# Adding up softmax exponentials on other engines: two accumulating DMAs at every odd step, no GpSimd addition, and VectorE's addition placed one step later

## The chip, the core and the metric

The kernel runs on one core of a Trainium2 chip: TensorE (PE; its weight loads are listed as PEld), VectorE (DVE), ScalarE (ACT), GpSimd (POOL) and SyncE (SP), each with its own queue of instructions in program order, and 16 DMA engines. The metric is device time in microseconds (us) of one launch. Before the change three runs took 2907.7, 2908.85 and 2916.73 us; the median is 2908.85 us.

## The reference

Two "metaformer" layers over an input of 2 x 256 x 64 x 64. Layer 0 has an area attention and a recurrence, layer 1 a set of small convolutions with a state-space scan and a mixture of experts. The change is in layer 0's attention alone:

```python
B, C, H, W = x.shape                        # 2, 256, 64, 64
N, hd = H * W, C // HEADS                   # 4096, 32 (HEADS = 8)
qk = _conv1x1_bn(x, w_qk, ...)
vv = _conv1x1_bn(x, w_v, ...)
pp = depthwise 5x5 convolution of vv, then batch norm
Ba, Na = (B * AREA, N // AREA)              # 8 areas of 1024 positions
...
attn = jnp.einsum('bhdn,bhdm->bhnm', q, k) * hd ** (-0.5)
attn = jax.nn.softmax(attn, axis=-1)
o = jnp.einsum('bhdm,bhnm->bhdn', v, attn)
...
return _conv1x1_bn(o + pp, w_proj, ...)
```

In each of 8 areas and 8 heads, 1024 queries attend to 1024 keys. The softmax needs, for each query, the sum of the exponentials over all 1024 keys; how this sum is put together is what changes.

## The kernel before

**Groups and steps.** A group is one area and one half of the channels (4 heads): 16 groups, 0 to 15. Each group has 16 steps t. A step handles 512 queries (`n`, the half) and 128 keys (`m`, 0 to 7), for 4 heads. The loop over all 256 steps (L567) writes the instructions out by hand in their final order; tables (`MINE`, `SMALL`, `LATE`, `AROUND`, `TAPS` and others) say which other work goes in at which step. Within a step the order is:

1. `scores` (L366): TensorE makes the scores in two PSUM tiles of two heads each (L371, L376), ScalarE takes their exponentials into two SBUF tiles of 128 x 1024 f32 (L383). They are named `sx0`, `sx1` at each fourth step (m = 0 and 4) and `ex0`, `ex1` at the others; each name has two buffers in turn.
2. `values` (L393) of the step before: TensorE multiplies its exponentials with v (L389, `av_o`).
3. `maxima` (L270) of the group to come: TensorE makes scores (L276); at even steps ScalarE stores their positive part (L288), at odd steps VectorE reduces against it (L292, four instructions). Three PSUM buffers of two banks are shared by 1 and 3.
4. The additions of exponentials, described below.
5. The taps of the 5 x 5 convolution on VectorE (L346), one to three a step.
6. Small work by table: projections for the next group (L166), their evictions, the layer norm's steps for the next area (`centre`, `square`, `variance`, `root`, `scale`), the output projection (L359), and at t = 15 `key_difference` (L264), a GpSimd subtraction of two key tiles that the next group's first `maxima` needs as `kd`. `join` (L308, L309) runs on GpSimd at t = 7 and 15. `root` (at t = 6 of a group with the first half of the channels, an "even group") is a transpose on VectorE (L199, `ln_t`), then an addition and a power on GpSimd (L202, L203); its second part comes at t = 8.

**The sums of exponentials.** Four steps (m = 0 to 3, or 4 to 7) are added into one pair of tiles, `total`, which are the `sx` tiles of the first of them. Two steps after the fourth, `sums` (L404) multiplies `total` by ones on TensorE (L389, `po`), which adds over the 128 keys; of each half of the queries, `sums` runs twice (two quads), and after the second VectorE normalises `y` (L415 to L423). Who adds what, before:

| step | first tile (heads 0 and 1) | second tile (heads 2 and 3) |
|---|---|---|
| m = 0, 4 | is the total | is the total |
| m = 1, 5 | accumulating DMA (L591) | GpSimd addition (L593) |
| m = 2, 6 | accumulating DMA | VectorE addition (L600), after the step's taps |
| m = 3, 7 | accumulating DMA | GpSimd addition |

An accumulating DMA reads `exs[0]` (512 KB), adds it to `total[0]` and writes it back. It is issued from GpSimd's queue, which stands still until the DMA before it on the same tile has landed. The GpSimd addition carries two extra waits (L595, L596), on the last score matmul of `maxima` and on the latest marked VectorE instruction before it, so that it starts beside VectorE's reductions, which read PSUM. `mark` records, all over the code, which VectorE instruction came last.

Of the kernel before, what the change touches and what calls it, by code (L numbers as in the profile page):

```python
# [14 lines left out]
ALU = mybir.AluOpType  # L15
# [78 lines left out]
def area_attention(tc, sh, ap):  # L94
# [9 lines left out]
    nc, x = tc.nc, sh.x  # L104
# [3 lines left out]
    with ExitStack() as ctx:  # L108
# [12 lines left out]
        w = {}  # L121
# [12 lines left out]
        held, xns, vhs, vts, qs, ks, kds, mxs, accs, ys, nms = ({} for _ in range(11))  # L134
# [4 lines left out]

        minus_half = cp.tile([P, 1], F32, name="minus_half")  # L140
        nc.gpsimd.memset(minus_half, -0.5)
        latest = [None]

        def mark(op):

            latest[0] = op.ins

        def wide():
            return ps1.tile([P, 2, 512], F32, name="ps", tag="ps")

# [3 lines left out]
        def temp(name, A):  # L154

            if (name, A) not in held:
                if early[0] is not None and A == 0:
                    held[name, A] = early[0].tile([P, NA], F32, name=name)
                else:
                    held[name, A] = p3.tile([P, NA], F32, name=name, tag="tmp")  # L160
            return held[name, A]
# [8 lines left out]
        def area(A):  # L170
            b, a = AREAS[A]
            return x[:, :, b, a * NA : (a + 1) * NA]
# [11 lines left out]
        def centre(A, c, at=FULL):  # L184
            if A not in xns:
                xns[A] = p1.tile([P, 2, NA], F32, name="xn")
            mark(nc.vector.tensor_tensor(xns[A][:, c, at], area(A)[:, c, at], temp("pm", A)[:, at], ALU.subtract))

        def square(A, c, at=FULL):
            nc.scalar.activation(temp(f"sq{c}", A)[:, at], xns[A][:, c, at], AF.Square)  # L190
# [4 lines left out]
        def root(A, part, at=FULL):  # L195
            n = (at.stop - at.start) // 32
            if part == 0:
                turned = temp("ln_t", A)[:, at]
                mark(nc.vector.transpose(turned, temp("var", A)[:, at]))  # L199
                t = turned.rearrange("p (k i) -> p k i", i=32)[:, :, 0]  # L200
                y = held["root", at.start] = p1.tile([P, NA // 32], F32, name="root")[:, :n]
                nc.gpsimd.tensor_scalar(y, t, 1e-6, None, ALU.add)  # L202
                nc.gpsimd.tensor_tensor(y, y, minus_half.to_broadcast([P, n]), ALU.pow)  # L203
            else:
                y = held.pop(("root", at.start))
                mark(nc.vector.transpose(
                    temp("ln_r", A)[:, at].rearrange("p (k i) -> p k i", i=32),
                    y.unsqueeze(2).to_broadcast([P, n, 32]),
                ))

        def scale(A, c, at=FULL):
            mark(nc.vector.tensor_tensor(xns[A][:, c, at], xns[A][:, c, at], temp("ln_r", A)[:, at], ALU.mult))

        def columns(t):
            return lambda k: t[:, k]
# [112 lines left out]
        def taps(A):  # L328

            vh, a = vhs[A], AREAS[A][1]  # L330
            for lower in range(2):
                for c in range(2):
                    if not lower:
                        acc = accs[A, c] = p1.tile([P, AROWS, WW], F32, name=f"acc{c}")
                        nc.vector.tensor_scalar(
                            acc, vh[:, c, 2 : 2 + AROWS], w_pe[:, c, 12:13], t_pe[:, c : c + 1], ALU.mult, ALU.add
                        )
                        yield
                    for k in range(25):
                        dy, dx = k // 5 - 2, k % 5 - 2  # L340
                        if dy == 0 and dx == 0 or (dy > 0) != lower:
                            continue
                        r0, r1 = window(dy, AROWS, AROWS * a, HH)
                        w0, w1 = window(dx, WW)
                        part = accs[A, c][:, r0:r1, w0:w1]
                        mark(nc.vector.scalar_tensor_tensor(  # L346
                            part, vh[:, c, 2 + r0 + dy : 2 + r1 + dy, w0 + dx : w1 + dx],
                            w_pe[:, c, k : k + 1], part, ALU.mult, ALU.add,
                        ))
                        yield  # L350

        def add_taps(A, c):
            y = ys[A, c]
            mark(nc.vector.tensor_tensor(y, y, accs.pop((A, c)).rearrange("p r w -> p (r w)"), ALU.add))

        def output(A, co, half):
            ps, to = bank(), area(A)[:, co, HALVES[half]]
            project(w["wpr"], co, lambda k: ys[A, k], half, ps)
            mark(nc.vector.scalar_tensor_tensor(to, ps, s_pr[:, co : co + 1], to, ALU.mult, ALU.add))  # L359

        def shift(A, co):

# [41 lines left out]
        def sums(G, n, half, exs):  # L404

            ps = bank()
            for h in range(GH):
                on_columns(ps, h, ones, exs, True, True)
            if half == 0:
                held["sum"] = p1.tile([P, 512], F32, name="sum")  # L410
                nc.scalar.copy(held["sum"], ps)
                return

            y, total = ys[GROUPS[G]][:, HALVES[n]], held.pop("sum")
            nc.vector.tensor_tensor(total, total, ps, ALU.add)  # L415
            turned = exs[0][:, 0]
            nc.vector.transpose(turned, total)
            small = p1.tile([P, 512 // 32], F32, name="small")
            nc.vector.reciprocal(small, turned.rearrange("p (k i) -> p k i", i=32)[:, :, 0])
            nc.vector.transpose(  # L420
                total.rearrange("p (k i) -> p k i", i=32), small.unsqueeze(2).to_broadcast([P, 512 // 32, 32])
            )
            mark(nc.vector.tensor_tensor(y, y, total, ALU.mult))  # L423

# [135 lines left out]
                    f(at, *a)  # L562

        pending, due, total = None, {}, None
        at_end = mybir.DependencyInfo(mybir.DependencyClass.Sync, mybir.DependencyReason.DATA)
        conv = iter(())
        for g in range(16 * len(GROUPS)):  # L567
            G, t = divmod(g, 16)
# [12 lines left out]
                values(*pending)  # L581
            works(G, t, SMALL_FIRST if new else SMALL, {})

            mm, before = None, latest[0]
            for k, at in (AHEAD_FIRST if new else AHEAD).get(t, ()):
                if G + k < len(GROUPS):
                    mm = maxima(G + k, at)
            if m % 4 == 0:
                total = exs
            else:  # L590
                nc.gpsimd.dma_start(total[0], exs[0], accum_op=ALU.add)  # L591
            if m % 2:
                add = nc.gpsimd.tensor_tensor(total[1], total[1], exs[1], ALU.add)  # L593
                if mm is not None:
                    tc.add_manual_dep(add.ins, mm.name, at_end, reason="beside the reductions")  # L595
                    tc.add_manual_dep(add.ins, before.name, at_end, reason="beside the reductions")  # L596
            for _ in range((TAPS_FIRST if A == 0 else TAPS)[c][t]):
                next(conv, None)
            if m % 4 == 2:
                mark(nc.vector.tensor_tensor(total[1], total[1], exs[1], ALU.add))  # L600
            works(G, t, FIRST if new else MINE, AROUND[c])
            if g in due:
                sums(*due.pop(g))
# [1719 lines left out]
```

## Time and profile before

| | |
|---|---|
| median of three runs | 2908.85 us |
| profiled execution | 2907.71 us, of it span 2905.9 us |
| attention, first score block to last output | about 62 to 1402 us of the span |
| PE busy, whole span | 2650.5 us (91%) |
| DVE / ACT / POOL busy | 1991.1 (69%) / 1562.2 (54%) / 1289.3 us (44%) |
| DMA queue 0 (issued from GpSimd) | 53056 packets, 225.88 MB, 30.5% of 16 engines |
| mean step in attention, from the first score blocks (L371) at 62.2 and 1375.2 us | (1375.2 - 62.2) / 255 = 5.15 us |
| accumulating DMA (L591), issue to landing | 4.5 / 4.6 / 6.3 us, min / median / max |
| GpSimd addition (L593) | 2337 / 2480 / 3080 ns |
| VectorE addition (L600) | 1215 / 1218 / 1312 ns |
| VectorE tap (L346) | 1115 / 1269 / 6770 ns |

"Busy" leaves out waiting, but a busy PE is not one at its peak. A line such as `L593 POOL TENSOR_TENSOR sx<-sx,ex ... x128 | 324.5, 2535 | 12.3 <-PE ...` reads: line, engine, operation, output and inputs, shape, how many; busy us in all and mean ns of one; idle time of the engine just before, and what ended it. In the timeline a line has start us, duration us (of a run of like instructions merged, with their count at the end), engine, line; in brackets the idle time before it and who ended it.

### The profile page before, as it was taken

What the parts mean: (1) busy time and instruction counts of PE and PEld (TensorE: products, weight loads), DVE (VectorE), ACT (ScalarE), POOL (GpSimd) and SP (SyncE); (2) the same over time, 40 slices, a digit from 0 to 9 for tenths busy, and PEclk for the clock granted to TensorE, in tenths of its full rate; (3) what the DMA queues carried; (4) which work ended last, traced back from release to release, by engine and by line L of the source; (5) the groups of instructions that cost most, each with busy time, mean ns of one, the idle gap of its engine ahead of it and who ended that gap; (6) DMA issues with size and microseconds to landing.
All of it is one profiled execution on the core that took longest, in us unless ns stands there. A gap on an engine that the chain in (4) does not pass through costs nothing.

```text
span 2905.9 us, 45896 instructions
## 1 busy us (share of the span) xinstructions
PE 2650.5 (91%) x17286; PEld 1490.6 (51%) x17286; DVE 1991.1 (69%) x3765; ACT 1562.2 (54%) x2641; POOL 1289.3 (44%) x1115
## 2 busy tenths in 40 slices
PE   7999999999999999998799999968886599999994
PEld 2223333333333333222599999933343488888873
DVE  4789888888888888879566666788897622222116
ACT  3667676676767676665244555567645522222223
POOL 1454545444554545445213000058772166666651
PEclk9999999999999999998799999989998799999995
DMA  3333443434343434445231000035552366666658
GB/s 131 66 73 74 80 81 73 81 74 81 75 79 74 80 73 81 78 79 100 80 126 65 1 1 2 1 86 150 143 149 94 113 216 232 220 229 229 221 177 348
DMA packets 86393, 321.04 MB, mean 110 GB/s; under 512 B 17608, under 2 KB 18512, under 8 KB 76432
## 3 DMA queue, kind: packets, MB, share of 16 engines
q0 software_dynamic: 53056, 225.88, 30.5%
q1 hardware_dynamic: 31872, 87.86, 9.4%
q10 hardware_dynamic: 1232, 4.25, 0.4%
q8 instruction: 139, 2.28, 0.3%
q14 instruction: 94, 0.77, 0.1%
HBM read 173.30 MB, written 43.58 MB: 75 GB/s over the span
## 4 chain that ended last, share of the span: by engine, by line
PE 74%; DVE 10%; issue 5%; DMA 4%; POOL 4%; ACT 3%; SPq 0%; DVEq 0%; POOLq 0%; ACTq 0%
PE ps L276 9%; PE ph L2069 9%; PE py L2079 8%; PE av_o L389 7%; PE z L796 7%; PE po L166 7%; PE z L808 7%; PE ps L376 6%; PE ps L371 3%; DMA sx<-ex 2%; DVE hs L1541 2%; PE yp L1551 2%; PE po L178 2%; PE po L389 2%; PE px L2057 1%
## 5 line engine op out<-in xcount | busy, mean ns | idle before, releaser
L346 DVE SCALAR_TENSOR_TENSOR acc<-vh,w_pe,acc 128x1008 f32<-128x1008 f32 (+7 forms) x384 | 534.0, 1393 | 9.5
L383 ACT ACTIVATE ex<-ps 128x1024 f32<-128x1024 f32 x384 | 372.8, 1024 | 177.2 <-PE ps L376 101.9
L591 POOL DMA_DIRECT2D sx<-ex x192 | 167.9, 875 | 594.6 <-ACT ex L383 273.5
L292 DVE CUSTOM_DVE_ANT_0 more<-ps,more 128x512 f32<-128x512 f32 x480 | 303.0, 687 | 154.6 <-PE ps L276 146.0
L2071 ACT ACTIVATE act<-ph,wt 128x256 f32<-128x256 f32 x272 | 128.8, 474 | 386.1 <-PE ph L2069 381.9
L593 POOL TENSOR_TENSOR sx<-sx,ex 128x1024 f32<-128x1024 f32 x128 | 324.5, 2535 | 12.3 <-PE ps L276 6.9
L2059 DVE COPY xt<-px 128x512 f32<-128x512 f32 x68 | 47.1, 692 | 396.7 <-PE px L2057 396.7
L2069 PE MATMUL ph<-xt,wt 128*128 128x256 f32 x1088 | 291.7, 391 | 4.7 <-ACT act L2071 3.0
L376 PE MATMUL ps<-q,k 32*128 32x512 f32 x2048 | 290.9, 607 | 0.0
L2079 PE MATMUL py<-wt,act 128*128 128x256 f32 x1088 | 278.8, 379 | 0.0
L288 ACT ACTIVATE more<-ps 128x1024 f32<-128x1024 f32 x240 | 233.1, 1025 | 30.3 <-ACT rows L320 7.8
L2069 PEld LDWEIGHTS ph<-xt,wt 128*128 128x128 f32 x1088 | 190.7, 191 | 67.0 <-DVE xt L2059 23.5
L796 PE MATMUL z<-xs,u 128*128 128x128 f32 x1872 | 224.5, 277 | 0.0
L796 PEld LDWEIGHTS z<-xs,u 128*128 128x128 f32 x1872 | 218.2, 194 | 0.2 <-issue 0.2
L2079 PEld LDWEIGHTS py<-wt,act 128*128 128x128 f32 x1088 | 202.0, 190 | 24.5
L820 ACT ACTIVATE t<-z,bias 128x128 f32<-128x128 f32 x468 | 136.3, 362 | 145.6 <-PE z L808 145.4
L389 PE MATMUL av_o<-ex,vt 128*32 128x512 f32 x1536 | 208.7, 613 | 0.2 <-ACT ex L383 0.2
L2094 POOL DMA_INDIRECT results<-y,ri x136 | 138.0, 1015 | 138.4 <-DVE y L2087 116.4
L276 PE MATMUL ps<-k,q 32*128 32x512 f32 x1088 | 186.5, 640 | 1.4 <-DVE nm L282 0.7
L808 PE MATMUL z<-xs,v 128*128 128x128 f32 x1512 | 180.1, 276 | 0.1
L808 PEld LDWEIGHTS z<-xs,v 128*128 128x128 f32 x1512 | 174.3, 192 | 0.7 <-DVE xs L827 0.7
L1548 POOL TENSOR_TENSOR cs<-hs,cs 128x1024 f32<-128x1024 f32 x63 | 148.9, 2365 | 54.4 <-DVE hs L1541 33.5
(431 smaller groups left out, 4535.8 us busy)
## 6 DMA issues: line engine op xcount, KB each, us to landing
sx<-ex POOLq DMA_DIRECT2D x192, 512.0 KB, 4.6
cs<-c_rows SPq DMA_DIRECT2D x128, 256.0 KB
y<-results SPq DMA_DIRECT2D x32, 512.0 KB
x<-xrows SPq DMA_DIRECT2D x8, 1024.0 KB
rows<-xt SPq DMA_DIRECT2D x16, 512.0 KB
out_x<-res POOLq DMA_DIRECT2D x15, 512.0 KB, 7.0
xrows<-xn SPq DMA_DIRECT2D x24, 256.0 KB
x<-in_x SPq DMA_DIRECT2D x4, 1024.0 KB
```

The lines of the kernel that those rows point to most:

```text
L276: mm = nc.tensor.matmul(tiles[h // 2][:, h % 2], qs[G, i // HM][head(h), i % HM * P : (i % HM + 1) * P], keys[head(h)], start=True, stop=T ...
L288: nc.scalar.activation(held["more"][j], tiles[j], AF.Relu)
L292: nc.vector.tensor_tensor_reduce(more, tiles[h // 2][:, h % 2], more, -1.0, 3.0e38, ALU.add, ALU.min, accum_out=nms[G][:, 0, h, i : i + 1],)
L346: mark(nc.vector.scalar_tensor_tensor(part, vh[:, c, 2 + r0 + dy : 2 + r1 + dy, w0 + dx : w1 + dx], w_pe[:, c, k : k + 1], part, ALU.mult, ...
L376: nc.tensor.matmul(tiles[h // 2][:, h % 2], k[head(h), m % HM * P : (m % HM + 1) * P], qs[G, n][head(h)], start=False, stop=True, tile_pos ...
L383: nc.scalar.activation(exs[i], tiles[i], AF.Exp, scale=HD**-0.5)
L389: nc.tensor.matmul(to[head(h)], lhs, exs[h // 2][:, h % 2], start=first, stop=last, tile_position=(0, HD * h))
L593: add = nc.gpsimd.tensor_tensor(total[1], total[1], exs[1], ALU.add)
L796: nc.tensor.matmul(z[c][:, g, :m], u[:, k, c, g], xt[:, k], start=g == GATES[0] and k == 0, stop=False, skip_group_check=True,)
L808: nc.tensor.matmul(z[c][:, g, :m], v[:, k, c, g], h[:, k], start=False, stop=k == 1, skip_group_check=True,)
L2069: nc.tensor.matmul(ph[:, hc], wt[:, at : at + P], xt[:, c], start=c == 0, stop=c == 1)
L2079: nc.tensor.matmul(py[:, j], act[:, hc, j * P : j * P + P], wt[:, at : at + C], start=hc == 0, stop=hc == NH - 1,)
```

## The change

GpSimd adds nothing any more. At odd m both tiles go by accumulating DMA, at m = 2 and 6 only the first. The second tile of m = 2 and 6 is still added by VectorE, but one step later: at the start of step m = 3 or 7, ahead of that step's `maxima` and after everything that VectorE has to do in the step before. `pending[3]` are the exponentials of the step before. The extra waits, `mark` and `latest` go with the GpSimd additions; taking away `mark(...)` around the other VectorE instructions changes none of them.

| step | first tile | second tile |
|---|---|---|
| m = 1, 5 | DMA | DMA |
| m = 2, 6 | DMA | (VectorE, in the next step) |
| m = 3, 7 | DMA | VectorE adds step 2's, then DMA adds step 3's |

```diff
-        latest = [None]
-
-        def mark(op):
-
-            latest[0] = op.ins
-
...
-        at_end = mybir.DependencyInfo(mybir.DependencyClass.Sync, mybir.DependencyReason.DATA)
...
-            mm, before = None, latest[0]
+            if m % 4 == 3:
+                nc.vector.tensor_tensor(total[1], total[1], pending[3][1], ALU.add)
             for k, at in (AHEAD_FIRST if new else AHEAD).get(t, ()):
                 if G + k < len(GROUPS):
-                    mm = maxima(G + k, at)
+                    maxima(G + k, at)
             if m % 4 == 0:
                 total = exs
-            else:
-                nc.gpsimd.dma_start(total[0], exs[0], accum_op=ALU.add)
-            if m % 2:
-                add = nc.gpsimd.tensor_tensor(total[1], total[1], exs[1], ALU.add)
-                if mm is not None:
-                    tc.add_manual_dep(add.ins, mm.name, at_end, reason="beside the reductions")
-                    tc.add_manual_dep(add.ins, before.name, at_end, reason="beside the reductions")
+            for i in ((), (0, 1), (0,), (0, 1))[m % 4]:
+                nc.gpsimd.dma_start(total[i], exs[i], accum_op=ALU.add)
             for _ in range((TAPS_FIRST if A == 0 else TAPS)[c][t]):
                 next(conv, None)
-            if m % 4 == 2:
-                mark(nc.vector.tensor_tensor(total[1], total[1], exs[1], ALU.add))
             works(G, t, FIRST if new else MINE, AROUND[c])
```

More of the change, by code (lines that the diff above doesn't have):

```diff
@@ L186, in centre @@
                 xns[A] = p1.tile([P, 2, NA], F32, name="xn")
-            mark(nc.vector.tensor_tensor(xns[A][:, c, at], area(A)[:, c, at], temp("pm", A)[:, at], ALU.subtract))
+            nc.vector.tensor_tensor(xns[A][:, c, at], area(A)[:, c, at], temp("pm", A)[:, at], ALU.subtract)
         def square(A, c, at=FULL):
@@ L198, in root @@
                 turned = temp("ln_t", A)[:, at]
-                mark(nc.vector.transpose(turned, temp("var", A)[:, at]))
+                nc.vector.transpose(turned, temp("var", A)[:, at])
                 t = turned.rearrange("p (k i) -> p k i", i=32)[:, :, 0]
@@ L205, in root @@
                 y = held.pop(("root", at.start))
-                mark(nc.vector.transpose(
+                nc.vector.transpose(
                     temp("ln_r", A)[:, at].rearrange("p (k i) -> p k i", i=32),
                     y.unsqueeze(2).to_broadcast([P, n, 32]),
-                ))
+                )
         def scale(A, c, at=FULL):
-            mark(nc.vector.tensor_tensor(xns[A][:, c, at], xns[A][:, c, at], temp("ln_r", A)[:, at], ALU.mult))
+            nc.vector.tensor_tensor(xns[A][:, c, at], xns[A][:, c, at], temp("ln_r", A)[:, at], ALU.mult)
         def columns(t):
@@ L345, in taps @@
                         part = accs[A, c][:, r0:r1, w0:w1]
-                        mark(nc.vector.scalar_tensor_tensor(
+                        nc.vector.scalar_tensor_tensor(
                             part, vh[:, c, 2 + r0 + dy : 2 + r1 + dy, w0 + dx : w1 + dx],
                             w_pe[:, c, k : k + 1], part, ALU.mult, ALU.add,
-                        ))
+                        )
                         yield
@@ L353, in add_taps @@
             y = ys[A, c]
-            mark(nc.vector.tensor_tensor(y, y, accs.pop((A, c)).rearrange("p r w -> p (r w)"), ALU.add))
+            nc.vector.tensor_tensor(y, y, accs.pop((A, c)).rearrange("p r w -> p (r w)"), ALU.add)
         def output(A, co, half):
@@ L358, in output @@
             project(w["wpr"], co, lambda k: ys[A, k], half, ps)
-            mark(nc.vector.scalar_tensor_tensor(to, ps, s_pr[:, co : co + 1], to, ALU.mult, ALU.add))
+            nc.vector.scalar_tensor_tensor(to, ps, s_pr[:, co : co + 1], to, ALU.mult, ALU.add)
         def shift(A, co):
@@ L422, in sums @@
             )
-            mark(nc.vector.tensor_tensor(y, y, total, ALU.mult))
+            nc.vector.tensor_tensor(y, y, total, ALU.mult)
         with ExitStack() as own:
```

## The prediction

> **What bounds the kernel now.** I read the busy times by stage first, then the costliest groups, the waits of TensorE, and last the timeline at the places where TensorE waits. Attention runs from about 62 us to 1400 us. The columns of the first view are the stretch, then busy time (and count) of PE, PEld, DVE, ACT and POOL, the granted clock, the DMA engines' busy share and GB/s.
>
> ```profile
> 100.00:1317.00 1217.00, 1181.88 (x7752) 368.47 (x7746) 1030.12 (x1602) 837.77 (x960) 602.72 (x463) 1.00 0.41 77
> 1317.00:1402.00 85.00, 64.07 (x387) 16.89 (x386) 69.91 (x65) 33.87 (x38) 37.10 (x26) 0.82 0.43 81
> ```
>
> Up to 1317 us TensorE is busy for 97% of the time at full clock: it is the bound, and at most 1217 - 1182 = 35 us can be won there, whatever happens on POOL. In the last group of 16 steps (1317 to 1402) it is busy for 75%, at a clock of 0.82: something else sets the pace.
>
> ```profile
> L346 DVE SCALAR_TENSOR_TENSOR acc<-vh,w_pe,acc 128x1008 f32<-128x1008 f32 (+7 forms) x384 | 534.0, 1393 | 9.5
> L591 POOL DMA_DIRECT2D sx<-ex x192 | 167.9, 875 | 594.6 <-ACT ex L383 273.5
> L593 POOL TENSOR_TENSOR sx<-sx,ex 128x1024 f32<-128x1024 f32 x128 | 324.5, 2535 | 12.3 <-PE ps L276 6.9
> ```
>
> The 128 POOL additions (L593) take 324.5 us of POOL. The taps of VectorE (L346) average 1393 ns, their median is 1269: (1393 - 1269) x 384 = 48 us lie in a few long ones, up to 6770 ns, and those stand beside POOL's two-input work. VectorE is busy for 85%, so this costs only where TensorE then waits:
>
> ```profile
> PE ps L371 <- ACT more L288: 11.9, 23, 1.0
> PE ps L371 <- DVE nm L292: 11.4, 21, 2.2
> PE po L389 <- DMA sx<-ex: 9.9, 4, 4.6
> PE ps L276 <- POOL kd L264: 9.8, 11, 2.0
> ```
>
> Us in total, times, longest. The first two return at the same steps of every group, where a step has no projection to fill the time from the last score block to its reduction, and VectorE itself waits for TensorE just before (0.7 to 1.6 us in the timeline): no addition on POOL stands in that loop. The last two can move: `kd` behind POOL's queue, and `sums` behind the accumulating DMAs.
>
> **The change part by part.** The third of each four steps has the hardest ending. At the boundary of groups 8 and 9 (start us, duration, engine, line):
>
> ```profile
> 825.03 0.85 POOL L591 DMA_DIRECT2D sx<-ex  x1 [2.45 <-DVE nm L292]
> 825.61 2.67 POOL L593 TENSOR_TENSOR sx<-sx,ex 128x1024 f32<-128x1024 f32 x1
> 827.93 1.55 POOL L264 TENSOR_TENSOR kd<-k,k 128x512 f32<-128x512 f32 x1
> 829.54 1.14 PE L276 MATMUL ps<-kd,q 32*128 32x512 f32 x8 [1.99 <-POOL kd L264]
> ```
>
> 1. *POOL's additions go, 128 DMA issues come.* An odd step spends 0.87 us (L591) in place of 2.54 (L593): 128 x 1.67 = 213 us less of POOL, which lie in POOL's idle time but for what queues behind them. That is `kd` at t = 15. ScalarE had its input (k, L247) ready at 826.18; POOL came 1.75 us later. Over the 13 boundaries into groups 2 to 14, `kd` starts 0.93, 0.88, 0.63, 1.75, 0.32 and 0.38 us after its key where POOL is late, and 0.07 to 0.08 elsewhere: 4.4 us late in sum. With two issues of 0.87 in place of 0.87 + 2.3 all are on time but this one, which keeps about 0.6: **-3.8 us**. Bounds: 0, if the DMA before it lands later by as much; -8.4, all that step 0 takes over its shortest (5.37 us), if the part that comes from taps holding up `kd` itself (1.36 us undisturbed, up to 2.29) went as well.
>
> 2. *VectorE is no longer held by L593.* Up to 1317 us I cost the 48 us at 0: VectorE's freed time turns into more waiting for TensorE. If that cover were gone, it is case C below. Behind 1317 us VectorE is the end of the chain, and it counts (part 5).
>
> 3. *Two accumulating DMAs in one step.* The DMA view for 200 to 1500 us (packets, MB, share of 16 engines; count, size, us to landing):
>
> ```profile
> q0 software_dynamic: 25200, 91.76, 37.3%
> sx<-ex POOLq DMA_DIRECT2D x175, 512.0 KB, 4.6
> ```
>
> 0.373 x 1300 / 175 = 2.77 us of all 16 engines each, 4.6 us to landing. So engines are free for 4.6 - 2.8 = 1.8 us of each, and a second one issued 0.87 us behind the first lands between 0.87 + 4.6 = 5.5 us (beside it) and 4.6 + 2.8 = 7.4 us (after it). No pair is in this trace; I take 7.0, near the upper end, because all go through queue 0. Occupancy goes from 3 x 2.77 = 8.3 to 13.9 us per four steps of 4 x 5.15 = 20.6 us: it fits. Whom does the second landing delay? ScalarE's exponential two steps later, which overwrites the tile: two steps last 8.8 to 11 us, free. VectorE's addition, which waits for it: it comes some 10 us after the issue, free. The next DMA on the first half waits only for the first landing, and starts moving 0.3 to 0.5 us later behind the rest of the second; its slack against `sums` is over 9 us. `sums` two steps after the third: over 8.6 us after the issue at t = 3, 11 and 15, free at 7.0 to 7.9. At t = 7 of even groups it is not free:
>
> ```profile
> 778.69 1.22 DVE L600 TENSOR_TENSOR sx<-sx,ex 128x1024 f32<-128x1024 f32 x1
> 781.16 0.32 POOL L202 TENSOR_SCALAR root<-ln_t 128x32 f32<-128x32 f32 x1 [4.41 <-DVE ln_t L199]
> 781.56 5.45 POOL L203 TENSOR_TENSOR root<-root,minus_half 128x32 f32<-128x32 f32 x1
> 786.98 0.93 POOL L591 DMA_DIRECT2D sx<-ex  x1
> 792.31 1.07 PE L389 MATMUL po<-sx,ones 128*32 128x512 f32 x8
> ```
>
> The power (L203) holds the DMA back, and `sums` follows 5.0 to 5.3 us after it in six groups. Its matmuls on the second half come 0.5 us later, so 5.5 to 5.8 are there for 7.0.
>
> 4. *VectorE's addition a step later.* The same 64 instructions of 1.22 us. At most steps nothing of VectorE's stands between the old and the new place, so it runs at the same time, ahead of the same reductions. At t = 6 of even groups the transpose `ln_t` stands there and goes ahead: the power begins about 1.0 us earlier (778.7 + 1.2 = 779.9 against 781.07). With part 3: 7.0 - 5.6 - 1.0 = 0.4 us in each of six groups: **+2 us** (0 by 5.5; 7.4 - 5.4 = 2.0 each, +12, if the transpose doesn't move). Queued behind the addition are the odd step's reductions, which free PSUM for TensorE; they start when TensorE has made their input, 0.4 to 2 us after the addition's end. At t = 3, 7, 11, 15 the second DMA waits for the addition, and POOL's `kd` and `join` queue behind that; the addition at t = 14 ended at 822.4, the issue would come at 825.9: covered.
>
> 5. *The last group.* It has no reductions, steps are short, and the chain runs DMA after DMA to 1355 us, then along VectorE:
>
> ```profile
> 1338.86 1.93 PE L389 MATMUL po<-sx,ones 128*32 128x512 f32 x8 [4.58 <-DMA sx<-ex]
> 1364.03 11.70 DVE L346 SCALAR_TENSOR_TENSOR acc<-vh,w_pe,acc 128x930 f32<-128x930 f32 x5
> 1383.71 3.36 DVE L354 TENSOR_TENSOR y<-y,acc 128x1024 f32<-128x1024 f32 x1
> ```
>
> On VectorE, 11.70 for five taps of 1.2 is 5.6 too long (one is the tap of 6.8), 3.36 for an addition of 1.22 is 2.1: -7.7 behind 1355 us. Against it, `sums` at t = 5 and t = 9 wait for a landing up to 2.4 us later each: +4.8, so VectorE's last stretch begins later by that. The end's `sums` has 9 us in hand (the last DMA lands at 1384.5, its use is at 1393.4), which the later chain may use up without a cost. Sum -7.7 + 4.8 = **-3 us**; bounds -7.7 (pairs land side by side) and +6, if a later landing is paid at all four sums (4 x 2.4 = 9.6) and half of VectorE's gain is lost behind it.
>
> A rule speaks against more issues from POOL. The Trainium skill, "SBUF — State Buffer", section "SBUF: two separate sides", says that GpSimd can't write a DMA's descriptors while VectorE runs in a two-port mode. Here 192 issues took 850 to 1207 ns, median 874; by the rule an issue could also wait out an operation such as L335 (818 ns), and for 15 of those the sum would be up to 12 us of POOL time, hidden; by the rows nothing.
>
> Sum: -3.8 + 2 - 3 = **-4.8 us**. The profiled execution took 2907.7 us (span 2905.9 and 1.8 around it), so it would take 2902.9; it lies 1.1 under the median of the three runs, 2908.85, from which the sum gives **2904 us**.
>
> **Rivals.** *A, forecast:* 2895 to 2909, chance 0.60. *B, the pairs get in each other's way:* the landing at t = 7 of even groups takes 9 us or more, `sums` waits over 2 us, and then the matmuls run slow: after the wait of 2.18 us at 202 us the next three took 2.31, 1.94 and 2.09 us instead of 1.24, 1.06 and 1.26 (+2.8). Six times 2.2 + 2.8 = 30 if all, half of it 15; less `kd`'s 3.8, with the last group at +4: about **2924**. It decides from 2 us of wait on. For it: no pair in the trace, and one queue. Against: 8 us of slack everywhere else. 0.18. *C, VectorE's freed time reaches TensorE:* a third of its 48 us plus part 1: **2889**. For it: TensorE's 23 us of waits for freed PSUM. Against: VectorE idles just before most of those. 0.14. *D, what `kd` wins the sums take back:* **2909**, within 1 us; the additions were off the path. 0.08.
>
> **How the numbers follow.** 0.3% (8.7 us) is about what a measurement of this kernel can tell. A straddles that bound: of its 0.60, 0.24 lie below 2900. Faster 0.24 + 0.14 = 0.38; slower B's 0.18; same 0.44. The range of 8 in 10 takes C's and B's nearer ends: 2887 to 2918; A's own is 2895 to 2909.
>
> **What would show it.** L593 gone, 320 issues at L591 of about 0.87 us; second landings 5.5 to 7.4 us after the first issue; taps' mean near 1270 ns; TensorE's wait for `kd` about 5 us in place of 9.8; step times elsewhere unchanged. Wrong, if VectorE's additions show waits for a DMA, if DMA landings exceed 9 us, or if TensorE waits for `sums` at every fourth step.

## The result, and the profile after

The changed kernel takes 2930.63 us (median of five runs, 2924.85 to 2931.59) against 2908.85 us before; the ratio is 1.0068, 95% interval 1.0049 to 1.0086. It is slower by about 22 us, where 2904 was forecast and 2887 to 2918 was the range. The profiled execution took 2930.63 us, of it span 2928.8 (before: 2907.71 and 2905.9).

Lines moved up by 6 in most of the code: the first score matmul is L365 (was L371), the second L370, the matmuls of `values` and `sums` L383, the taps L340, `kd` L258, VectorE's addition L578, the accumulating DMA L585, the transpose and the power of `root` L193, L196 and L197.

The busy times by stretch, of the changed kernel (stretch, then PE, PEld, DVE, ACT, POOL with counts, granted clock, share of the DMA engines, GB/s); the last group now lies at 1331 to 1420 us:

```profile
100.00:1317.00 1217.00, 1177.07 (x7680) 365.98 (x7680) 983.29 (x1588) 829.17 (x952) 416.02 (x458) 1.00 0.67 126
1331.00:1420.00 89.00, 68.29 (x388) 16.88 (x387) 58.02 (x65) 33.90 (x38) 24.00 (x29) 0.87 0.69 130
```

POOL gave up 187 us of work in the first stretch, VectorE 47, and TensorE, the bound, is busy for a little less than before (1177 for 1182, with 1% fewer matmuls in the stretch: 7680 for 7752). The DMA engines went from 0.41 to 0.67. Everything that was to become lighter did, and the time rose.

The costliest groups after (busy us, mean ns | idle time before them):

```profile
L585 POOL DMA_DIRECT2D sx<-ex x320 | 279.7, 949 | 812.3 <-ACT ex L377 418.8
L340 DVE SCALAR_TENSOR_TENSOR acc<-vh,w_pe,acc 128x1008 f32<-128x1008 f32 (+7 forms) x384 | 483.4, 1261 | 9.5
```

TensorE's waits in attention after, 100 to 1400 us (us in total, times, longest):

```profile
PE po L383 <- DMA sx<-ex: 20.9, 13, 3.5
PE ps L365 <- ACT more L282: 12.0, 23, 1.0
PE ps L365 <- DVE nm L286: 11.4, 21, 2.2
PE ps L270 <- POOL kd L258: 9.1, 13, 0.8
```

The two waits that were said to have nothing to do with POOL stand as they were (11.9 and 11.4 before). The one for `kd` fell by 0.7 only. The matmuls of `sums` wait for a landing 13 times in place of 4.

The DMA view of 200 to 1500 us after (packets, MB, share of 16 engines; count, size, us to landing):

```profile
q0 software_dynamic: 42208, 153.64, 62.7%
sx<-ex POOLq DMA_DIRECT2D x292, 512.0 KB, 5.4
```

0.627 x 1300 / 292 = 2.79 us of the engines each, as before; only the landing is later. In the trace, 123 of the 128 pairs were given out together (issues under 1.3 us apart). Their second DMA landed 7.3 us after the first issue in the median, 2.6 us behind the first DMA; 52 of the 123 took more than 7.4 us: 50 of them up to 9.0, and two in the last group 10.4 and 10.6.

**Where the time went.** I set the starts of the 256 steps (the first score block of each) of the two traces side by side. Of the 208 steps from group 2 to 14, all agree within 0.05 us on the mean of their kind but two kinds: t = 0, and t = 9 with 10 of the even groups, where `sums` of t = 7 runs. Each row below gives what a stretch took more than in the first trace before, in us; the last two columns are whole durations. The last group is counted from its first score block (1315.47 us before) to the first transpose behind attention (1402.59): 87.1 us. Some expectations below count it 0.5 us longer (87.6 before, 91.0 after); the differences are the same. The runs of the next section are in it already; the kernel before and the changed one were traced twice.

| kernel | ratio, 95% interval | groups 0, 1 | t = 0 | t = 9, 10 even | other steps | last group | attention | behind it |
|---|---|---|---|---|---|---|---|---|
| before | | 0 | 0 | 0 | 0 | 0 (87.1) | 1340.4 | 1503.3 |
| before, again (e12) | 0.9993 [0.9984, 1.0003] | -2.5 | +1.5 | +1.0 | +0.1 | -3.1 | 1337.4 | 1507.8 |
| after | 1.0068 [1.0049, 1.0086] | +0.2 | -1.2 | +13.1 | +0.4 | +3.3 | 1356.3 | 1508.9 |
| after, again (e7) | 1.0062 [1.0046, 1.0078] | +0.2 | -1.1 | +13.2 | +0.4 | +3.2 | 1356.1 | 1510.0 |
| e1 | 1.0122 [1.0101, 1.0144] | -2.7 | -1.2 | +13.4 | +11.0 | +2.8 | 1363.7 | 1515.3 |
| e2 | 1.0019 [1.0008, 1.0030] | -2.5 | -0.5 | 0.0 | +0.3 | +0.6 | 1338.2 | 1511.7 |
| e3 | 1.0043 [1.0028, 1.0059] | +0.4 | -1.1 | +13.0 | +0.4 | -1.2 | 1351.8 | 1502.7 |
| e4 | 1.0051 [1.0034, 1.0068] | -4.2 | -0.9 | +5.6 | +1.2 | +3.8 | 1345.9 | 1512.7 |
| e5 | 1.0003 [0.9991, 1.0015] | -2.4 | -1.1 | +3.6 | +0.3 | -4.2 | 1336.6 | 1508.9 |
| e6 | 0.9998 [0.9985, 1.0011] | -2.5 | +3.0 | 0.0 | 0.0 | -3.4 | 1337.5 | 1503.3 |
| e9 | 1.0033 [1.0022, 1.0045] | -2.8 | +6.0 | 0.0 | +0.1 | +1.4 | 1345.0 | 1508.1 |
| e10 | 1.0008 [0.9997, 1.0018] | -2.5 | +3.4 | +1.0 | 0.0 | +2.4 | 1344.7 | 1513.7 |
| e13 | 1.0085 [1.0071, 1.0099] | +1.9 | -1.2 | +22.0 | +0.4 | +4.1 | 1367.6 | 1506.2 |
| e14 | 1.0083 [1.0069, 1.0098] | +1.9 | -1.2 | +20.6 | +0.3 | -4.1 | 1358.0 | 1507.4 |
| e15 | 1.0037 [1.0020, 1.0053] | 0.0 | -1.1 | +3.1 | +0.4 | +4.4 | 1347.1 | 1509.6 |
| e16 | 0.9996 [0.9983, 1.0009] | -3.0 | -1.2 | +2.1 | +0.3 | +1.9 | 1340.5 | 1506.1 |

From the means of the two traces each, the span grew by 22.9 us (2929.4 against 2906.5): 17.3 of them in attention, of which 12.7 are t = 9 and 10 of even groups, 4.8 the last group, 1.4 groups 0 and 1, and -1.9 t = 0. The rest is 1.7 ahead of attention and 3.9 behind it, where the instructions are the same. The last group scatters: seven traces with pairs in it took 87.7 to 91.5 us, mean 90.3, and four without (before, e12, e6, e9) 83.8 to 88.5, mean 85.9. So its loss is some 4 us on the mean, and a single trace doesn't give it. In groups 0 and 1, t = 9 and 10 of group 0 cost 1.7 us more as well; the small sum hides it behind 2.8 us in group 1, which the last section takes up.

**t = 7 of an even group, after.** The timeline of the changed kernel in group 8 (start us, duration, engine, line):

```profile
788.14 1.25 DVE L193 STREAM_TRANSPOSE ln_t<-var 128x1024 f32<-128x1024 f32 x1
789.31 1.18 DVE L578 TENSOR_TENSOR sx<-sx,ex 128x1024 f32<-128x1024 f32 x1
789.48 1.20 POOL L196 TENSOR_SCALAR root<-ln_t 128x32 f32<-128x32 f32 x1 [3.35 <-DVE ln_t L193]
790.76 5.45 POOL L197 TENSOR_TENSOR root<-root,minus_half 128x32 f32<-128x32 f32 x1
796.18 1.84 POOL L585 DMA_DIRECT2D sx<-ex  x2
...
801.60 1.05 PE L383 MATMUL po<-sx,ones 128*32 128x512 f32 x4
803.45 1.05 PE L383 MATMUL po<-sx,ones 128*32 128x512 f32 x4 [0.79 <-DMA sx<-ex]
```

The transpose did go ahead of VectorE's addition. But POOL's small instruction L196 now runs beside that addition and takes 1.20 us in place of 0.32, in all seven places of the trace, so the power begins only 0.1 us earlier in its step (0 to 0.3 us in the six groups). The pair is issued at 796.18, lands at 800.80 (4.6 us) and 803.40 (7.2 us), and TensorE starts on the second half at 803.45. The eight matmuls of `sums` now span 801.60 to 804.50, 2.9 us where they took 1.07. Four of them alone take 1.05 us, as long as the eight took together. So all the time from 801.60 to the start of the second half, 1.84 us, is lost, and step 9 lasts 6.26 us in place of 4.43; in the six groups with a `root` it lasts 6.26 to 8.16. Step 10 gives 0.33 back in five of them (5.40 us in place of 5.73). In group 6 the pair itself landed later, 5.2 and 8.6 us after the first issue in both traces; no run shows why. The wait is longest there, and the matmuls behind it run slow:

```profile
634.95 1.40 PE L383 MATMUL po<-sx,ones 128*32 128x512 f32 x4 [2.26 <-DMA sx<-ex]
636.27 0.61 PE L365 MATMUL ps<-mx,ones_b 3*128 3x512 bf16 x4
636.68 1.92 PE L370 MATMUL ps<-q,k 32*128 32x512 f32 x8
```

The 1.92 is 1.03 elsewhere; the granted clock from 635 to 642 us is 0.76.

**`kd`, after**, at the boundary of groups 8 and 9:

```profile
834.36 1.75 POOL L585 DMA_DIRECT2D sx<-ex  x2 [2.22 <-ACT ex L377]
836.60 5.75 DVE L340 SCALAR_TENSOR_TENSOR acc<-vh,w_pe,acc 128x868 f32<-128x868 f32 x4
837.05 1.83 POOL L258 TENSOR_TENSOR kd<-k,k 128x512 f32<-128x512 f32 x1 [0.95 <-ACT k L241]
```

POOL is free 0.95 us before the key is ready, so the queue is no longer what `kd` waits for. But `kd` itself takes 1.83 us beside VectorE's taps (1.55 here before, 1.36 undisturbed; the median of its 15 went from 1.58 to 1.96), and TensorE waits for it 0.7 us at each of the 13 boundaries.

**The last group.** The longest pieces of the chain that ended last, after, 1325 to 1425 us (start us, us, what):

```profile
1338.67 7.41 DMA sx<-ex
1349.95 6.52 DMA sx<-ex
1368.82 6.78 DMA sx<-ex
1385.07 6.63 DMA sx<-ex
1404.42 6.59 DMA sx<-ex
```

Before, the same view held three DMA pieces of 4.55 to 5.56 us, a tap of 6.78 and the output matmuls. The tap is gone from it, as forecast, but VectorE's gain met a wait:

```profile
1384.46 6.13 DVE L340 SCALAR_TENSOR_TENSOR acc<-vh,w_pe,acc 128x930 f32<-128x930 f32 x5
...
1400.15 1.22 DVE L348 TENSOR_TENSOR y<-y,acc 128x1024 f32<-128x1024 f32 x1
1413.02 0.69 DVE L409 TENSOR_TENSOR sum<-sum,po 128x512 f32<-128x512 f32 x1 [6.97 <-PE po L383]
```

Five taps take 6.13 us (11.70 before) and L348 1.22 (3.36), all 7.7 us came, and then VectorE stands for 6.97 us until the sums behind the last pair are there. That pair was issued at 1403.88 and its second DMA landed at 1411.01; the second half of the sums started at 1411.06. Over the group TensorE waited for landings 8 times, 17.2 us in all, where it waited 3 times and 9.7 us before. Steps are short here, so pairs meet on the queue: those of t = 3 and t = 5 were issued in one run,

```profile
1349.15 3.63 POOL L585 DMA_DIRECT2D sx<-ex  x4 [4.23 <-ACT sx L377]
```

and the fourth of these landed at 1361.64, 10.6 us after the first issue of its own pair.

### The profile page after: what moved, and what is told of

Its sections match the earlier page's. It is cut to its first block, busy times and chain, and to the rows that moved or that the text cites. A ratio compares the mean times of both kernels' runs of the same rounds, so it can differ in the third digit from the quotient of the medians.

```text
span 2928.8 us, 45921 instructions
## 1 busy us (share of the span) xinstructions
PE 2668.0 (91%) x17286; PEld 1493.5 (51%) x17286; DVE 1942.8 (66%) x3765; ACT 1562.8 (53%) x2641; POOL 1089.4 (37%) x1115
## 4 chain that ended last, share of the span: by engine, by line
PE 65%; DVE 10%; issue 9%; DMA 8%; POOL 4%; ACT 3%; SPq 0%; POOLq 0%; DVEq 0%; ACTq 0%
PE ph L2056 9%; PE py L2066 8%; PE ps L270 7%; PE z L783 7%; DMA sx<-ex 7%; PE z L795 7%; PE av_o L383 6%; PE ps L370 5%; PE po L160 5%; PE ps L365 2%; PE yp L1538 2%; DVE hs L1528 2%; PE po L172 1%; PE po L383 1%; DVE more L286 1%
## 5 line engine op out<-in xcount | busy, mean ns | idle before, releaser
L585 POOL DMA_DIRECT2D sx<-ex x320 | 279.7, 949 | 812.3 <-ACT ex L377 418.8
L340 DVE SCALAR_TENSOR_TENSOR acc<-vh,w_pe,acc 128x1008 f32<-128x1008 f32 (+7 forms) x384 | 483.4, 1261 | 9.5
L286 DVE CUSTOM_DVE_ANT_0 more<-ps,more 128x512 f32<-128x512 f32 x480 | 303.0, 687 | 182.5 <-PE ps L270 172.2
L370 PE MATMUL ps<-q,k 32*128 32x512 f32 x2048 | 289.4, 606 | 0.0
L383 PE MATMUL av_o<-ex,vt 128*32 128x512 f32 x1536 | 209.7, 613 | 0.5 <-ACT ex L377 0.5
L365 PE MATMUL ps<-mx,ones_b 3*128 3x512 bf16 x1024 | 139.7, 387 | 26.3 <-ACT more L282 12.0
```

The source lines that it names most:

```text
L286: nc.vector.tensor_tensor_reduce(more, tiles[h // 2][:, h % 2], more, -1.0, 3.0e38, ALU.add, ALU.min, accum_out=nms[G][:, 0, h, i : i + 1],)
L340: nc.vector.scalar_tensor_tensor(part, vh[:, c, 2 + r0 + dy : 2 + r1 + dy, w0 + dx : w1 + dx], w_pe[:, c, k : k + 1], part, ALU.mult, ALU.add,
L370: nc.tensor.matmul(tiles[h // 2][:, h % 2], k[head(h), m % HM * P : (m % HM + 1) * P], qs[G, n][head(h)], start=False, stop=True, tile_pos ...
L383: nc.tensor.matmul(to[head(h)], lhs, exs[h // 2][:, h % 2], start=first, stop=last, tile_position=(0, HD * h))
L585: nc.gpsimd.dma_start(total[i], exs[i], accum_op=ALU.add)
```

## The experiments

The theory after the traces: in attention the change costs what the second landing of a pair comes too late, at two places only: t = 9 of the even groups, where POOL's power holds the pair back, and the last group. The rivals: more DMA traffic slows everything a little; VectorE's addition stands in the wrong place; the additions' going is itself harmful. Edits are against the changed kernel unless the kernel before is named.

**The two places, each undone alone.** e2 gives the second half of step 7 in even groups back to POOL, e3 that of the last group.

```diff
             for i in ((), (0, 1), (0,), (0, 1))[m % 4]:
-                nc.gpsimd.dma_start(total[i], exs[i], accum_op=ALU.add)
+                if i == 1 and t == 7 and c == 0:             # e3: G == len(GROUPS) - 1
+                    nc.gpsimd.tensor_tensor(total[1], total[1], exs[1], ALU.add)
+                else:
+                    nc.gpsimd.dma_start(total[i], exs[i], accum_op=ALU.add)
```

> The changed kernel, but at t = 7 of even groups GpSimd adds the second tile, as before the change; the other 120 pairs of DMAs stay. 'The pair behind the power': GpSimd's addition of 2.5 us ends before the first tile's DMA lands (4.6 us), so TensorE's waits at t = 9 go: 2916 us (2912 to 2920). 'Load': 8 of 128 additional DMAs go, 1/16 of the loss, 2929 us. 'The move': unchanged, 2930 us.

> The changed kernel, but in the last group GpSimd adds the second tile at odd steps, as before the change; VectorE's addition stays in its new place. In the first trace the last group takes 91.0 us in place of 87.6. 'Second landings' (each quad of the last group waits 2 to 3 us more for the second tile): the sums at t = 5, 9 and 13 come 2 us earlier each, but VectorE is held by GpSimd again; last group 86 to 88 us, time 2926 us. Rival 'load' (128 more DMAs slow every step a little): 8 of 128 go, 2929 us, and the last group stays at 91 us.

e2: 2913.92 us; t = 9 and 10 are back at 0.0 with 8 instructions changed of 128, and no wait of `sums` is left up to 1320 us. The 312 DMAs that remain, and the 120 additions that stay away, don't show in any other step: against the rival of traffic and against that of the additions' going. e3: 2919.76 us; the last group falls by 4.5 us to 85.9 and t = 9 keeps its 13.0. Its time is 6 us under what was expected; the stretch behind attention, where nothing was changed, is the shortest of all traces.

**Less traffic in the pair.** e5 lets the second DMA move one of its two heads; the kernel leaves the odd steps' exponentials of the other head out of its sum, so it is of use for its times alone:

```diff
+                part = slice(0, 1) if i else slice(0, 2)
-                nc.gpsimd.dma_start(total[i], exs[i], accum_op=ALU.add)
+                nc.gpsimd.dma_start(total[i][:, part], exs[i][:, part], accum_op=ALU.add)
```

> The changed kernel with the second DMA of each pair cut to half its size (256 KB): the odd steps' exponentials of the fourth head of each group are left out of its sum. 'Second landings': the second one moves 1.4 us less behind the first and lands about 5.8 us after the first's issue in place of 7.2. Steps at t = 9 of even groups 6.4 -> 5.0 us, 7 x 1.4 = 10 us, and 2 to 4 us in the last group: 2917 us. 'Load': the additional traffic is halved, so half of the 22 us spread over all steps: 2919 us, and the steps other than t = 9 change. The table of steps tells these two apart, not the time.

2909.14 us, 8 us under what was expected: t = 9 keeps 3.6 of its 13.1 us and the last group takes 82.9, with as many instructions in every queue as in the changed kernel. The size of the second transfer carries most of the loss, not the issue.

**VectorE's addition.** e6 moves it one step later in the kernel before; e4 puts it, at t = 7 alone, behind the reductions, so that it no longer runs beside L196.

```diff
-            if m % 4 == 3:
+            if m % 4 == 3 and t != 7:
                 nc.vector.tensor_tensor(total[1], total[1], pending[3][1], ALU.add)
             for k, at in (AHEAD_FIRST if new else AHEAD).get(t, ()):
                 if G + k < len(GROUPS):
                     maxima(G + k, at)
+            if t == 7:
+                nc.vector.tensor_tensor(total[1], total[1], pending[3][1], ALU.add)
```

> The kernel before, with VectorE's addition alone moved one step later; GpSimd's additions stay and no DMA is added. 'The move': as much of the loss as it causes, up to 2930 us. 'The pair behind the power' and 'load': 2909 us (2905 to 2913); the step at t = 9 of even groups stays at 4.4 us.

> The changed kernel, but at t = 7 of every group VectorE's addition stands behind the step's reductions and not ahead of them. In the changed kernel GpSimd's L196 takes 1.20 us in place of 0.32, beside VectorE's addition, and so the power begins no earlier than before although its transpose ended 1.0 us earlier. 'The move': with the addition out of the way L196 takes 0.32 us again, the power, both DMAs and the sums at t = 9 come 0.9 us earlier, 7 x 0.9 = 6 us: 2924 us. 'The pair behind the power' allows the same, but no more: 0.6 to 0.9 us a group stay as waits at t = 9. 'Load': 2930 us.

e6: 2909.25 us, no difference: without pairs the move costs nothing. e4: 2923.15 us, t = 9 down from 13.1 to 5.6. Its timeline in group 8:

```profile
784.66 0.32 POOL L196 TENSOR_SCALAR root<-ln_t 128x32 f32<-128x32 f32 x1 [3.63 <-DVE ln_t L193]
785.07 5.45 POOL L197 TENSOR_TENSOR root<-root,minus_half 128x32 f32<-128x32 f32 x1
790.49 1.84 POOL L587 DMA_DIRECT2D sx<-ex  x2
```

L196 is back at 0.32 us and the power lies nearly 0.9 us earlier against its step. So over half of the 13 us (13.1 - 5.6 = 7.5) hangs on that overlap, and a pair without it is still too late. e6 has the overlap too (L202 took 1.19 to 1.20 us there), and without a pair it costs nothing.

**Giving the landing time: expectations that missed.** e1 runs the sums of t = 7 one step later:

```diff
-                due[g + 2] = G, n, m // 4, total
+                due[g + (3 if t == 7 and c == 0 else 2)] = G, n, m // 4, total
```

> The changed kernel, but in the even groups the sums of the quad that ends at t = 7 run three steps after it (t = 10) and not two (t = 9); nothing else moves. Theory 'the pair behind the power': the second DMA of t = 7 lands 7.2 us after the first's issue, which the power on GpSimd holds back, and TensorE waits for it at t = 9: 1.5 to 1.8 us in groups 0, 2, 4, 8, 10 and 12 and 4.5 us in group 6, 15 us in all. These steps fall back to 4.4 us and the time to 2916 us (2912 to 2920). Rival 'load' (128 more DMAs slow every step a little): nothing changes, 2930 us. Rival 'the move' (VectorE's addition in its new place costs it): nothing changes, 2930 us.

2943.66 us, slower still. The wait moved from the landing to a PSUM bank, which VectorE's L353 frees (timeline of group 8), and, by more, to VectorE's reductions (L286), for which TensorE waits 27.1 us in place of 11.4 (waits of 100 to 1400 us):

```profile
805.29 0.75 DVE L353 SCALAR_TENSOR_TENSOR x<-po,pr_s,x 128x512 f32<-128x512 f32 x1 [3.17 <-PE po L160]
806.10 1.06 PE L383 MATMUL po<-sx,ones 128*32 128x512 f32 x8 [0.84 <-DVE x L353]
```

```profile
PE ps L365 <- DVE nm L286: 27.1, 35, 2.2
PE po L383 <- DVE x L353: 5.9, 7, 0.8
```

The sums at t = 9 stand where the bank is free; a step later the output projection has it. e10, the kernel before with the moved addition and sums three steps later in the last group alone, met the same bank, as its rival said:

> The kernel before; in the last group alone VectorE's addition is made one step later and the sums of a quarter three steps behind it in place of two. Theory (VectorE held by GpSimd's addition there, then the sums' wait for the landing): the last group falls from 87.6 us to 82-84.5, nothing else moves, 2902-2906 us, ratio 0.998-0.999. Rival (the sums then wait for the one bank, as they did at t=10 of the run that put the even groups' sums later): 87 us or more for the group, 2909 us or more.

2910.98 us: `sums` there waits 7.36 us for L359, and the group takes 89.5 us.

e13 keeps the sums and moves the power, from t = 6 to t = 7 (transpose left in place):

```diff
+        def power(A, at=FULL):          # the addition and the power of root, part 0
...
-            6: [(1, root, 0)],
+            6: [(1, root, 0)], 7: [(1, power)],
...
```

> The changed kernel, with the power on GpSimd (0.3 + 5.5 us) given out at t=7, behind that step's pair of DMAs, in place of t=6, ahead of it; VectorE's transpose stays where it is. Theory (the power holds the pair's issue back until 796.2 us of the profiled run, and the second landing, 7.2 us behind the first issue, is then too late for the sums): the pair is issued when the exponentials of t=7 end, at 790.8, and has landed by 798.5, before the sums are due at 800.2; t=9 and 10 of the six even groups lose their +13.1 us against the kernel before, and the time falls from about 2929 to 2915-2921 us (the upper end if the roots, about 1.5 us later, hold up VectorE). Rival (two DMAs in place of one cost the time wherever they are issued, by contention or by a slower clock): the steps stay at +10 us or more and the time stays at 2926-2931.

> The same, and in the last group alone the second DMA of an odd step is the addition on GpSimd again. Theory: both stretches that lost time are then mended; the last group falls from 91.0 to about 86.4 us, as in the run that had this part alone, and the time to 2906-2914 us, no longer measurably slower than before or barely so (0 to +0.2%). Rival (part of the loss belongs to the many DMAs themselves): 2918 us or more.

2934.8 and 2933.48 us, both missed. At t = 9 it went as the theory had it: 4.43 us in all six groups, no wait. But t = 10 took 7.9 to 10.8 us in place of 5.4 to 5.7:

```profile
803.04 1.04 POOL L306 CAST parts<-nm 128x16 bf16<-128x16 f32 x1 [0.98 <-DVE nm L290]
...
805.44 5.45 POOL L194 TENSOR_TENSOR root<-root,minus_half 128x32 f32<-128x32 f32 x1
810.92 1.25 DVE L204 STREAM_TRANSPOSE ln_r<-root 128x1024 f32<-128x1024 f32 x1 [2.30 <-POOL root L194]
...
814.70 0.61 PE L369 MATMUL ps<-mx,ones_b 3*128 3x512 bf16 x2 [2.12 <-DVE nm L290]
```

In that place the power queues behind the casts of `join` too, which wait for the next maxima. It ends at 810.9, VectorE waits 2.30 us for it, VectorE's reductions come late, and TensorE waits for them. My edit had moved two things at once.

**The power right behind the pair.** e15 mends that (`power` is as in e13, and out of `root`); e16 adds e3's edit.

```diff
                 nc.gpsimd.dma_start(total[i], exs[i], accum_op=ALU.add)
+            if t == 7 and c == 0 and A + 1 < len(AREAS):
+                power(A + 1)
```

> The changed kernel, with the power on GpSimd given out right behind the pair of DMAs of t=7, ahead of the casts that wait for the maxima of the next step (the run before this one put it behind those casts as well, where the power began 3 us later and VectorE's transpose waited 2.3 us for it). Theory (the power, lying ahead of the pair, is what makes the second landing too late): the sums of t=9 find both landings done, as they did in that run, and the power ends at the time at which it is wanted, so nothing is late at t=10 either: t=9 and 10 of the even groups -0.5 to +1 us against the kernel before instead of +13 and +22, time 2913-2917 us, ratio 1.002-1.004. Rival (the pair costs its time wherever it is put, in a slower clock or on the engines it takes from): t=9 and 10 still +6 us or more, 2922 us or more.

> The same, with the second DMA of an odd step replaced by the addition on GpSimd in the last group alone. Theory: the last group falls from 91 to 83.5-86.5 us as in the two runs that had this part; with t=9 mended too, attention takes 1335-1339 us (the kernel before: 1340.4 and 1337.4) and the time is 2905-2911 us, no different from the kernel before within what can be measured. Rival (something else of the change is left over): attention 1343 us or more, 2914 us or more.

e15: 2920.29 us, 3 above what was expected; e16: 2908.1 us, ratio 0.9996 [0.9983, 1.0009], the time that was expected, but not by the way that was expected: its last group took 89.0 us and attention 1340.5, both above their ranges (83.5 to 86.5 and 1335 to 1339) and below the rival's 1343. Against the kernel with pairs there, the last group fell in all three cases, by 4.5 (e3), 8.2 (e14 against e13) and 2.5 us (e16 against e15). The timeline of e15 in group 8:

```profile
781.34 1.75 POOL L589 DMA_DIRECT2D sx<-ex  x2 [4.61 <-ACT ex L381]
783.15 0.32 POOL L193 TENSOR_SCALAR root<-ln_t 128x32 f32<-128x32 f32 x1
783.56 5.45 POOL L194 TENSOR_TENSOR root<-root,minus_half 128x32 f32<-128x32 f32 x1
...
792.22 1.06 PE L387 MATMUL po<-sx,ones 128*32 128x512 f32 x8
```

The same pair, issued as soon as its exponentials are there, has 10.9 us until `sums`, which runs its eight matmuls in 1.06 us. Step 9 is 4.43 us in all six groups; the +3.1 left are 1.0 at t = 10 in each of three groups, where the step of before took 5.73 us and these 6.75 or 6.76. With both places mended the change is worth nothing either way; of the kernels that compute everything none beat the one before. TensorE's waits in e16 (100 to 1330 us) have no line for a landing:

```profile
PE ps L369 <- DVE nm L290: 13.5, 23, 2.2
PE ps L369 <- ACT more L286: 11.9, 23, 1.0
PE ps L274 <- POOL kd L262: 9.1, 13, 0.8
PE ps L274 <- ACT more L286: 0.2, 1, 0.2
```

**The kernels themselves again, and issues alone.**

> The changed kernel once more, as it is, for its trace: which of its losses come back. From the first trace: attention 15.9 us longer (first score block to the first transpose behind it), everything behind attention 5.6 us longer, the start 1.4 us later. 'The pair behind the power': the 1.5 to 2 us at t = 9 of even groups and the 3 us of the last group come back to 0.2 us. What lies behind attention has the same instructions in both kernels; if its 5.6 us are chance, they differ by some us from this run to the first.

> The kernel before, unchanged, for a second trace of it. If the stretch behind attention (1503.3 us in the first trace; 1502.7 to 1515.3 in the eight other kernels, which run the same instructions there) is a property of the kernel, it comes back within 1.2 us, as it did for the changed kernel (1508.9 and 1510.0). If it scatters from one execution to the next, it comes out anywhere from 1503 to 1512, and the 5.6 us between the two kernels behind attention are not the change's. Time 2905-2912 us either way.

> The kernel before, with an accumulating DMA of one column (128 x 4 bytes) more at each odd step, into a tile that nothing reads: as many DMAs and nearly as many packets as the changed kernel, with 1/1024 of the additional bytes. GpSimd issues 128 x 0.87 us more. 'Second landings' and 'the pair behind the power': the sums don't wait for these; kd starts up to 0.9 us later in some groups: 2909 to 2920 us, and what lies behind attention is as long as before. Rival 'queue place' (the number of DMAs on GpSimd's queue makes the rest of the program longer): the part behind attention grows by 5 to 9 us, as in the traces with pairs.

e7: 2928.26 us; every deviation of the first trace came back within 0.2 us in attention. e12: 2908.34 us, but its stretch behind attention is 4.5 us longer than in the first trace and its last group 3.1 shorter. So both stretches scatter by some us from one trace of a kernel to the next, which is the second outcome written down for e12. e9 (one one-column DMA more at each odd step, its target read by nothing): 2918.96 us. At t = 0 `kd` came 6.0 us later in sum behind the added issues, and the other steps stayed where they were: an issue costs where something short queues behind it on POOL. The rest of its 10 us lies behind attention in its trace (+4.8), within that scatter. The number of DMAs by itself doesn't make the rest of the program longer: e5 with 320 and e16 with 312 take as long as the kernel before.

## Why the prediction was wrong

- **What bounds it: right.** TensorE's clock and waits up to the last group decide; 187 us less of POOL and 47 less of VectorE (part 2's 48, costed at 0) won nothing there. Steps away from the named places agree with before, so part 3's "free" cases (exponential, VectorE's addition, sums of t = 3, 11 and 15) hold up to the last group, but for one wait of VectorE's addition of 0.4 us.
- **Part 1, `kd`, -3.8: too large.** t = 0 gained 1.2 to 2.7 us, by which trace of before it is set against. The queue's part went as said; the time of `kd` itself beside the taps, left as it was in the forecast, rose (median 1.58 to 1.96 us).
- **Part 3, the pair: right in its order, its upper bound too low.** One lands behind the other, 7.3 us after the first issue in the median, beside the 7.0 taken; but 52 of 123 took more than the bound of 7.4. At t = 7 of the six groups it was 7.2 to 7.6 us in five and 8.6 in group 6.
- **Parts 3 and 4 together, "7.0 - 5.6 - 1.0 = 0.4 us in each of six groups: +2 us": this step failed.** It measured +12.7. The time in hand from the first issue to `sums` was put at 5.6 + 1.0 = 6.6 us and was 5.3 to 5.4. The 1.0 was read from the transpose alone; 0 to 0.3 of it came, because L196 on POOL waits out the moved addition (0.32 to 1.20 us; e4 takes the overlap away and gets 7.5 us back). The 5.6 held 0.5 us because the matmuls on the second half "come 0.5 us later"; but the four of one half take 1.05 us alone and all eight took 1.07, so a second half that starts 0.5 us later ends 0.5 us later, and none of the 0.5 is to spare. So 1.8 to 2.0 us were to be paid in place of 0.4 in four groups, 2.3 and 3.3 in groups 12 and 6, where the pair landed at 7.6 and 8.6; t = 10 gave 0.33 back in five groups and cost 1.2 more in group 6, where matmuls ran slow. The upper bound of 2.0 each ("if the transpose doesn't move") came near by luck: the transpose moved, and the power hardly did.
- **Part 5, the last group, -3: sign wrong.** VectorE's 7.7 us came in full, but the four sums each waited for a pair, at the end too, where 9 us were said to be in hand: TensorE's waits for landings grew by 7.5 us, not 4.8. The part counted each pair alone; here they met on the queue and landed up to 10.6 us after their first issue. +3.3 and +3.2 in the two traces (+4.8 against the mean of two before), with the scatter named above; inside its bound of +6.
- **The rule on POOL's issues.** The prediction weighed it against the rows, and they decide: the 320 issues took 850 to 1223 ns, median 865, where the 192 before took 850 to 1207, median 874.
- **The rivals.** B's time (2924) was nearest, and its places right, t = 7 of even groups and the last group at +4. Its condition, a landing of 9 us there, was not met: a pair of 7.2 us behind the power was enough, with idle waits of 0.8 to 1.3 us in five of the six groups, and only in group 6 did the matmuls run slow behind it. The terms at their upper bounds (+12 and +6) give 2927 less what `kd` won: the range ended at 2918, short of the case in which two bounds come together.
- **The signs of being wrong.** Each of the three showed, in the last group: VectorE's addition waited 2.0 us for a DMA, two DMAs took 9.7 and 9.8 us to land, and TensorE waited for every `sums`.
- **Open.** The 1.7 us ahead of attention and 3.9 behind it. The stretch behind attention took 1502.7 to 1515.3 us in sixteen traces with the same instructions, and 4.5 us more in one trace of before than in the other; the eleven traces with pairs have a mean of 1509.0 and the four with no DMA added (before, e12, e6, e10) 1507.0. This scatter can hold the 3.9, but it is not shown that it does. Why the pair of group 6 lands late. e15 and e16 differ by 12 us in the medians where their traces show 6.6 in attention.

## What to carry to other kernels

Before an engine's work is given to a transfer, count the time from issue to use at each place where it is issued, with a pair counted as one behind the other, and look first at what lies ahead of the issue in its queue: here one 5.45 us power ahead of one step in 32 made most of the loss, and moving that, without taking back a DMA, mended that part. When an instruction moves, look at what it now runs beside on the other engine. And a place in an order written by hand may be there for a resource: sums a step later lost more to a bank and to late reductions than they won from the landing. Last, work whose second half has to wait may cost its whole time twice: here four matmuls took as long as eight.

## What the hardware showed that was not expected

- **A small POOL instruction beside a two-input VectorE addition** took 1.20 us in place of 0.32, at every one of its seven places (in e6 too; 0.32 in e4, where the addition stands elsewhere). The Trainium skill, "SBUF — State Buffer", section "Who interferes with whom", says that a VectorE instruction with both inputs in SBUF contends with a GpSimd instruction that reads SBUF. L196 and L578 agree with it: 789.48 + 1.20 = 790.68 lies 0.2 us behind the addition's end.
- **Two 512 KB accumulating DMAs issued together** landed 2.6 us apart in the median, close to the 2.79 us that one occupies the engines, and one alone took 4.6 us. The skill's "DMA: Bandwidth & Descriptors", section "Anatomy of one DMA — SWDGE (gpsimd) path", fits about 2.0 us plus the bytes at 436 GB/s, an estimate of 3.2 us here. The measured 4.6 decides for an accumulating one.
- **The clock after a wait of TensorE is not the same each time.** A wait of 2.18 us by the same matmuls of group 1 ends at 201.99 us in the first trace before and at 206.41 after; the first lines are of before, the last of after, over the 7 us behind it:

```profile
202.00:209.00 7.00, 7.00 (x32) 1.97 (x32) 6.03 (x8) 3.25 (x4) 5.89 (x5) 0.57 0.17 32
```

```profile
206.30:213.30 7.00, 6.60 (x52) 2.18 (x53) 6.14 (x10) 5.71 (x8) 4.87 (x5) 1.00 0.67 125
```

The granted clock is 0.57 in the one and 1.00 in the other; in the second trace of before it is 0.76. That is worth 2.8 us in group 1 between the first trace of before and that of after, and 1.3 between the two of before. It is not the change's: e15, with pairs, repeats the first trace of before (0.0), and e9, without, repeats after (-2.8). A step table over one trace each would have booked it as a gain.
